# Layer 3 of a four-layer graph network: the product with W2 as seven products of halves, a mean by transposes, and adj's halves in three buffers

## The chip, the cores and the metric

The kernel runs on one core of a Trainium2 chip. The metric is the device time of one execution in microseconds, taken as the median of several runs. A core has a matrix engine (TensorE, PE in the profile; its weight loads are shown as PEld), VectorE (DVE), ScalarE (ACT), GpSimd (POOL) and SyncE (SP), which issues most transfers. All of them run at once, each through its own list of instructions in order, and wait for one another by semaphores. A matmul multiplies a stationary block of 128 x 128 (the weights) with a moving block of 128 rows and up to 512 columns, and its result goes to PSUM.

## The reference, cut to what matters

There are 16 graphs of 1024 nodes with 256 features each. Four layers follow one another, and each has the form x = x + layer(relu(layernorm(x)), adj). The change concerns the last one only:

```python
def _L3_gnn_ref(x, adjacency, epsilon, W1, b1, rms_weight, W2, b2):
    neighbor_sum = jnp.einsum('bnm,bmd->bnd', adjacency, x)
    agg = epsilon * x + neighbor_sum
    h = jnp.einsum('bnd,dh->bnh', agg, W1) + b1            # 256 -> 1024
    h = jax.nn.silu(_rmsnorm(h, rms_weight))               # over the 1024
    out = jnp.einsum('bnh,hd->bnd', h, W2) + b2            # 1024 -> 256
    return out
...
h = jnp.maximum(_layernorm(x, axis=-1), 0.0)
x = x + _L3_gnn_ref(h, adj, ...)
```

All data are fp32.

## The kernel before

Layers 0 and 1 work graph by graph and take the first 1443 us or so. Layer 2 is a recurrence over the nodes; it is written in an order fixed by hand, goes on until about 3392 us, and loads the first things for layer 3 on its way (`early_3`). Neither of them is touched. Layer 3 (`layer_3`) works through the 16 graphs ("batches") b = 0 to 15 from there to the end.

For one batch, layer 3 does this. `load(b)` fetches x, the result hn of layer 2 and the transposed adjacency matrix, the last in two halves of 512 columns (2 MB each, four transfers), all through SP's queue. `prepare(b)` adds hn to x, takes the layer norm's statistics on VectorE (lines 1150 to 1154), the power -1/2 on GpSimd (line 83, a helper), the Relu on ScalarE (line 1160), adds epsilon to the diagonal of adj (GpSimd, line 1141) and b2 to x (GpSimd, line 1164). `sums(b)` computes the neighbour sums, turned (features down, nodes across), in four parts of eight matmuls of 512 columns (line 1176). ScalarE copies each into `ag` (line 1178) and VectorE makes the differences `tt` (lines 1182 to 1186).

`inner` multiplies with W1. That product is already computed by the Strassen-Winograd scheme: both matrices are cut into 2 x 2 blocks, and seven products of blocks replace the eight. W1's sums of blocks are in `ws`; those of `ag` are in `tt`. For each of four k there are seven matmuls of 512 columns (line 1197). p1 goes from PSUM to SBUF on ScalarE (line 1212), VectorE adds it and the further products up in u2 and u3 (lines 1214 and 1216), and `result` adds the bias and writes a block of `hh` (line 1201). `result` also squares the block on ScalarE (line 1203, two `sq` buffers) and adds the square to `ss` on GpSimd (line 1205). The last product of a k is accumulated in PSUM on top of p5 and so has to wait until VectorE has read p5. `hh` is kept turned: the 1024 features are in 8 chunks of 128 partitions, nodes 0 to 511 in `hh[0]`, the others in `hh[1]`.

`norm` gives two steps. `mean` sums `ss` over the partitions by eight matmuls with one moving column of ones (line 1231, two records each) and gets the reciprocal root rms (lines 81 and 83). `spread` spreads rms over the partitions by eight transposes (line 1239), multiplies `hh` by it on VectorE (line 1242) and applies Silu on ScalarE (line 1243). `outer(b, hh, q)` multiplies one half of the nodes with W2: for each of four blocks of 128 nodes there are eight matmuls of 256 columns with the block of `hh` as weights (line 1251), and VectorE adds the result to x (line 1252). The store of x goes through GpSimd's queue (line 1282).

The loop at the end of `layer_3` sets the order: in iteration b come `load(b + 2)`, `inner` of b, the first part of `sums(b + 1)`, `mean`, the second part, `spread`, the third and fourth part, `outer` of the first half, `prepare(b + 2)`, `outer` of the second half, the store. Outside of layer 2 this is only the order in which the program is written. The framework's scheduler makes each engine's list from it and may move an instruction ahead of others that it doesn't depend on; `tc.issue_after(last)` keeps `prepare(b + 2)` from being put ahead of an add of `outer`.

Buffers: x has three, hn two, each half of adj has one of four (even batches use the two named `bxt`, odd ones the two named `at`), `hh[0]`, `hh[1]`, `ag` and `tt` have one each. PSUM has eight banks of 512 fp32 columns: five named `ph` (sums and `inner`), three named `po` (mean, spread, `outer`).

Of the kernel before, what the change touches and what calls it, by code (L numbers as in the profile page):

```python
# [9 lines left out]
F32 = mybir.dt.float32  # L10
# [6 lines left out]
P = 128  # L17
# [23 lines left out]
def gnn_stack(ctx: ExitStack, tc: tile.TileContext, a: dict, out: bass.AP):  # L41
# [1009 lines left out]


    def early_3(shared, pool, x, hn, at, h):

# [36 lines left out]
    def layer_3(shared, x, hn, at, h, eye):  # L1091
        with ExitStack() as st:
# [26 lines left out]
            nc.gpsimd.tensor_tensor(ws[:, 2], a12, ws[:, 1], ALU.subtract)  # L1119

            def load(b):
                if b:
# [6 lines left out]
                while len(at[b]) < N // NH:  # L1129
                    n0 = NH * len(at[b])  # L1130
                    half = shared.tile([P, NT, NH], F32, name="bxt") if b % 2 == 0 else big.tile([P, NT, NH], F32, name="at")
                    for t in range(0, NT, 2):
                        nc.sync.dma_start(half[:, t : t + 2], rows(a["adjT"][b])[:, t : t + 2, n0 : n0 + NH])
                    at[b].append(half)

            def prepare(b):
# [25 lines left out]
                to = x[b] if b else big.tile([P, NT, D], F32, name="x", bufs=3)  # L1162
                for t in range(NT):
                    nc.gpsimd.tensor_tensor(to[:, t], x[b][:, t], b2, ALU.add)  # L1164
                x[b] = to
# [23 lines left out]
            def inner(ag, tt):  # L1189
# [5 lines left out]
                def product(lhsT, rhs, onto=None):  # L1195
                    ph = onto if onto is not None else psum.tile([P, NH], F32, name="ph", bufs=5)
                    nc.tensor.matmul(ph, lhsT, rhs, start=onto is None, stop=True, skip_group_check=onto is not None)  # L1197
                    return ph

                def result(k, q, ph, u):  # L1200
# [5 lines left out]
                    begun[q] = True  # L1206

                for k in range(HH):
                    mine = slice(k * P, (k + 1) * P)
                    p1, u2, u3 = (small.tile([P, NH], F32, name=name) for name in ("p1", "u2", "u3"))  # L1210
                    ph = product(a11[:, mine], ag[:, 0, :NH])
                    nc.scalar.copy(p1, ph)  # L1212
                    ph = product(ws[:, 1, mine], tt[:, 1])
                    nc.vector.tensor_add(u2, ph, p1)  # L1214
# [5 lines left out]
                    result(k, 0, product(a12[:, mine], ag[:, 1, :NH]), p1)  # L1220
                    result(k, 1, product(ws[:, 2, mine], ag[:, 1, NH:], p5), u2)
                return hh, ss

            def norm(hh, ss):
# [3 lines left out]
                def mean():  # L1228
                    pq = psum.tile([P, N // P], F32, name="po", bufs=3)
                    for n in range(N // P):  # L1230
                        nc.tensor.matmul(pq[:, n : n + 1], ss[n // 4][:, n % 4 * P : (n % 4 + 1) * P], ones[:, 0:1],  # L1231
                                         start=True, stop=True)
                    got["rms"] = inv_sqrt(small, pq, RMS_EPS, [P, N // P], "rms", mul=1.0 / H)

# [10 lines left out]

            def outer(b, hh, q):
                for k in range(NH // P):
                    t = q * NH // P + k
                    po = psum.tile([P, D], F32, name="po", bufs=3)
                    for c in range(HC):  # L1250
                        nc.tensor.matmul(po, hh[q][:, c, k * P : (k + 1) * P], w2[:, c], start=c == 0, stop=c == HC - 1)  # L1251
                    last = nc.vector.tensor_add(x[b][:, t], x[b][:, t], po)
                return last.ins

# [7 lines left out]
            for b in range(B):  # L1262
# [12 lines left out]
                parts[3]()  # L1275
                last = outer(b, hh, 0)
                if b + 2 < B:

                    with tc.issue_after(last):
                        prepare(b + 2)  # L1280
                outer(b, hh, 1)
                nc.gpsimd.dma_start(rows(out[b]), x[b])
# [53 lines left out]
```

## Time and profile before

| | us |
|---|---|
| three runs | 4754.09, 4754.99, 4761.2 |
| median | 4754.99 |
| the profiled execution | 4754.82 |
| its span in the profile | 4753.1 |
| one batch of layer 3 in the middle | 83.07 |
| of it `inner`, sums with mean and spread, `outer` | 25.31, 30.13, 27.63 |
| mean granted TensorE clock over the span | 0.979 |

The profile describes one execution. Times in it are microseconds from the start of the span unless marked ns. A row of instructions gives line, engine, operation, what it writes and reads, the shape and the count. An fp32 matmul shows as two records of weight load and matmul (here called passes), a transpose as one. The end of a matmul is modelled, and neighbouring matmuls overlap in the records, so the distance from one start to the next says more than the duration. "Releaser" or "waited for" names the instruction that ended an engine's idle time.

### The profile page before, as it was taken

The numbers are of one execution on the slowest core, as the hardware profiler recorded it, in microseconds if no ns is written. First come the engines' busy times: TensorE is split into PE (matmuls) and PEld (weight loads), VectorE is DVE, ScalarE is ACT, GpSimd is POOL, SyncE is SP. The second block draws the span as 40 slices with busy tenths as digits, with TensorE's granted clock in tenths as the row PEclk, the third lists the DMA queues.
The fourth block names the chain that finished last, engine by engine and source line by source line (L and its number), as shares of the span: only waits on it lengthen the run. The fifth ranks groups of instructions, "written<-read, shape, count | busy, mean of one in ns | idle before, by whom it ended". The sixth has DMA issues, their size and how long they took to land. (4 is left out here: it accounts for less than half of the span.)

```text
span 4753.1 us, 52478 instructions
## 1 busy us (share of the span) xinstructions
PE 4421.1 (93%) x18071; PEld 2991.8 (63%) x18071; DVE 2344.1 (49%) x6436; ACT 1271.5 (27%) x2725; POOL 1554.1 (33%) x1926
## 2 busy tenths in 40 slices
PE   8998799999997989999999999998899999999998
PEld 4444455555554777777777777777556565565656
DVE  6667844446543444444444444445344444444443
ACT  1111112212211232222332323233233333333232
POOL 3213224334322323232223233324343424333331
PEclk9999899999998999999999999999899999999999
DMA  4333234654546443545344454431422232222200
GB/s 147 123 107 106 79 83 160 207 187 160 177 138 195 129 150 123 159 135 165 110 139 139 120 161 148 154 130 37 149 80 90 79 106 80 96 91 80 93 23 18
DMA packets 530981, 576.62 MB, mean 121 GB/s; under 512 B 42545, under 2 KB 439473, under 8 KB 528305
## 3 DMA queue, kind: packets, MB, share of 16 engines
q1 hardware_dynamic: 499536, 460.27, 31.3%
q0 software_dynamic: 31040, 111.44, 6.7%
q8 instruction: 196, 3.21, 0.3%
q14 instruction: 209, 1.70, 0.1%
HBM read 469.65 MB, written 116.65 MB: 123 GB/s over the span
## 5 line engine op out<-in xcount | busy, mean ns | idle before, releaser
L295 PE MATMUL pa<-at,h 128*128 128x512 f32 x1088 | 497.0, 610 | 32.9 <-DVE ag L300 32.9
L1251 PE MATMUL po<-w,hh 128*128 128x256 f32 x2048 | 447.6, 381 | 0.7 <-ACT hh L1243 0.7
L623 PE MATMUL pf<-hb,ab 128*128 128x256 f32 x1568 | 418.6, 385 | 28.1 <-DVE bxt L773 16.2
L1251 PEld LDWEIGHTS po<-w,hh 128*128 128x128 f32 x2048 | 391.0, 191 | 61.2 <-issue 7.2
L295 PE MATMUL pa<-at,q 128*128 128x512 f32 x960 | 424.4, 595 | 0.0
L295 PEld LDWEIGHTS pa<-at,h 128*128 128x128 f32 x1088 | 209.8, 196 | 278.8 <-issue 233.0
L735 PE MATMUL pf<-hs,wx 128*128 128x256 f32 x1536 | 350.2, 382 | 16.7 <-POOL hs L726 15.1
L1205 POOL TENSOR_TENSOR ss<-ss,sq 128x512 f32<-128x512 f32 x224 | 279.9, 1269 | 165.5 <-ACT sq L1203 161.7
L735 PEld LDWEIGHTS pf<-hs,wx 128*128 128x128 f32 x1536 | 291.3, 192 | 60.0 <-POOL hs L726 16.9
L623 PEld LDWEIGHTS pf<-hb,ab 128*128 128x128 f32 x1568 | 277.1, 192 | 67.8 <-DVE bxt L773 23.5
L295 PEld LDWEIGHTS pa<-at,q 128*128 128x128 f32 x960 | 178.3, 190 | 216.5 <-issue 212.6
L770 PE MATMUL pf<-bd,h 128*128 128x384 f32 (+5 forms) x768 | 213.9, 372 | 49.5 <-DVE bxt L773 26.5
L1022 POOL DMA_INDIRECT hs_d<-h,table x128 | 129.6, 1012 | 368.8 <-ACT gates L743 183.3
L1176 PE MATMUL ph<-bxt,hb 128*128 128x512 f32 x512 | 226.0, 597 | 4.0 <-ACT hb L1160 3.2
L1176 PE MATMUL ph<-at,hb 128*128 128x512 f32 x512 | 224.3, 593 | 0.0
L773 DVE TENSOR_TENSOR bxt<-bxt,pf 128x384 f32<-128x384 f32 (+5 forms) x384 | 141.3, 384 | 145.0 <-PE pf L770 124.8
L1242 DVE TENSOR_TENSOR hh<-hh,po 128x512 f32<-128x512 f32 x256 | 154.4, 679 | 111.6 <-PE po L1239 111.6
L83 POOL TENSOR_TENSOR rs<-rs_v,mhalf 128x8 f32<-128x8 f32 (+1 forms) x65 | 106.9, 1644 | 279.9 <-DVE rs_v L79 266.4
L740 DVE TENSOR_TENSOR gates<-pf,bias 128x512 f32<-128x512 f32 x128 | 88.3, 691 | 220.1 <-PE pf L735 205.4
L1203 ACT ACTIVATE sq<-hh 128x512 f32<-128x512 f32 x224 | 141.1, 630 | 194.8 <-DVE hh L1201 128.4
L770 PEld LDWEIGHTS pf<-bd,h 128*128 128x128 f32 x768 | 132.4, 192 | 94.4 <-DVE bxt L773 41.8
L829 ACT ACTIVATE r<-pr 128x256 f32<-128x256 f32 (+3 forms) x230 | 68.1, 348 | 405.8 <-PE pr L788 382.1
(274 smaller groups left out, 7917.4 us busy)
## 6 DMA issues: line engine op xcount, KB each, us to landing
at<-in_adjT SPq DMA_DIRECT2D x64, 1024.0 KB
ab<-in_adj SPq DMA_DIRECT2D x128, 512.0 KB
bxt<-in_adjT SPq DMA_DIRECT2D x64, 512.0 KB
at<-in_adjT SPq DMA_DIRECT2D x64, 512.0 KB
ad<-in_adj SPq DMA_DIRECT2D x128, 128.0 KB
x_d<-x POOLq DMA_DIRECT2D x16, 1024.0 KB, 4.8
he_d<-h POOLq DMA_DIRECT2D x16, 1024.0 KB, 9.2
heT_d<-hT POOLq DMA_DIRECT2D x16, 1024.0 KB
```

What stands on the lines that cost most here:

```text
L83: nc.gpsimd.tensor_tensor(r, t, mhalf.to_broadcast(shape), ALU.pow)
L295: nc.tensor.matmul(pa, h[:, mt, c * P : (c + 1) * P], at[n0 // 512][:, mt], start=mt == 0, stop=mt == NT - 1)
L623: nc.tensor.matmul(pb, ab[:, jts[k]], hb[:, jts[k]], start=k == 0, stop=k == len(jts) - 1)
L735: nc.tensor.matmul(pg[:, e], wx[:, c, q * D + e * P : q * D + (e + 1) * P], self.hs[:, c], start=c == 0, stop=c == DC - 1)
L770: nc.tensor.matmul(pf, h[:, g, c * P : (c + 1) * P], bd[:, g, b4 : b4 + 4, S : S + far], start=True, stop=True)
L773: return lambda: nc.vector.tensor_add(to, to, pf)
L1022: nc.gpsimd.indirect_dma_start(out=hs_d[t][g][:, :], out_offset=row(1, g, t, s), in_=h[:, g], in_offset=None)
L1176: nc.tensor.matmul(pa, h[b][:, mt, c * P : (c + 1) * P], at[b][n0 // NH][:, mt], start=mt == 0, stop=mt == NT - 1)
L1203: nc.scalar.activation(sq, hh[q][:, k], AF.Square)
L1205: nc.gpsimd.tensor_tensor(ss[q], ss[q], sq, ALU.add)
L1242: nc.vector.tensor_mul(hh[q][:, k], hh[q][:, k], pr)
L1251: nc.tensor.matmul(po, hh[q][:, c, k * P : (k + 1) * P], w2[:, c], start=c == 0, stop=c == HC - 1)
```

## The change

The change has five parts.

1. `outer` handles both halves of the nodes together, as a 2 x 2 block product with seven products of blocks. A block of `hh` is 512 features by 512 nodes, a block of W2 is 512 features by 128 columns. W2's sums of blocks (`wt`, and v12 in place) are made once by four GpSimd instructions. The sums of `hh`'s blocks are made per batch on VectorE (`combine`, eight instructions of 1024 columns), three of them in place and one in a new buffer `s1`. A product is 16 matmuls of 128 columns. Results go to x from PSUM on VectorE (four adds of 512 columns) or by way of `p1`, `u2` and `u3` (one copy on ScalarE, two adds on VectorE, three on GpSimd).
2. `mean` turns `ss` by eight transposes into PSUM and sums with two VectorE reductions.
3. In `inner` the last product of a k, with its `result`, is written after the first product and the copy of p1 of the next k (`left`).
4. The 32 halves of adj go round three buffers (two `bxt`, one `at`) instead of four.
5. `prepare(b + 2)` is issued after the add of the third product in `outer`, and its b2 add takes two blocks at a time.

The diff, without a blank line that it adds near the top:

```diff
--- before.py
+++ after.py
@@ -1118,6 +1119,13 @@
             nc.gpsimd.tensor_tensor(a21, a11, a21, ALU.subtract)
             nc.gpsimd.tensor_tensor(ws[:, 2], a12, ws[:, 1], ALU.subtract)
 
+            wt = wp.tile([P, 3, HH, P], F32, name="wt")
+            v11, v12, v21, v22 = (w2[:, m * HH : (m + 1) * HH, e * P : (e + 1) * P] for m in range(2) for e in range(2))
+            nc.gpsimd.tensor_tensor(wt[:, 0], v12, v11, ALU.subtract)
+            nc.gpsimd.tensor_tensor(wt[:, 1], v22, wt[:, 0], ALU.subtract)
+            nc.gpsimd.tensor_tensor(v12, v22, v12, ALU.subtract)
+            nc.gpsimd.tensor_tensor(wt[:, 2], v21, wt[:, 1], ALU.subtract)
+
             def load(b):
                 if b:
                     x[b] = big.tile([P, NT, D], F32, name="x", bufs=3)
@@ -1128,7 +1136,11 @@
                     at[b] = []
                 while len(at[b]) < N // NH:
                     n0 = NH * len(at[b])
-                    half = shared.tile([P, NT, NH], F32, name="bxt") if b % 2 == 0 else big.tile([P, NT, NH], F32, name="at")
+
+                    if (2 * b + len(at[b])) % 3 < 2:
+                        half = shared.tile([P, NT, NH], F32, name="bxt")
+                    else:
+                        half = big.tile([P, NT, NH], F32, name="at", bufs=1)
                     for t in range(0, NT, 2):
                         nc.sync.dma_start(half[:, t : t + 2], rows(a["adjT"][b])[:, t : t + 2, n0 : n0 + NH])
                     at[b].append(half)
@@ -1160,8 +1172,8 @@
                     nc.scalar.activation(h[b][:, t], x[b][:, t], AF.Relu, bias=shift[:, k : k + 1], scale=rs[:, k : k + 1])
                 diagonal(1)
                 to = x[b] if b else big.tile([P, NT, D], F32, name="x", bufs=3)
-                for t in range(NT):
-                    nc.gpsimd.tensor_tensor(to[:, t], x[b][:, t], b2, ALU.add)
+                for t in range(0, NT, 2):
+                    nc.gpsimd.tensor_tensor(to[:, t : t + 2], x[b][:, t : t + 2], b2[:, None].to_broadcast([P, 2, D]), ALU.add)
                 x[b] = to
 
             def sums(b):
@@ -1205,11 +1217,13 @@
                         nc.gpsimd.tensor_tensor(ss[q], ss[q], sq, ALU.add)
                     begun[q] = True
 
+                left = lambda: None
                 for k in range(HH):
                     mine = slice(k * P, (k + 1) * P)
                     p1, u2, u3 = (small.tile([P, NH], F32, name=name) for name in ("p1", "u2", "u3"))
                     ph = product(a11[:, mine], ag[:, 0, :NH])
                     nc.scalar.copy(p1, ph)
+                    left()
                     ph = product(ws[:, 1, mine], tt[:, 1])
                     nc.vector.tensor_add(u2, ph, p1)
                     ph = product(a21[:, mine], tt[:, 2])
@@ -1218,7 +1232,9 @@
                     result(HH + k, 1, p5, u3)
                     result(HH + k, 0, product(a22[:, mine], tt[:, 3]), u3)
                     result(k, 0, product(a12[:, mine], ag[:, 1, :NH]), p1)
-                    result(k, 1, product(ws[:, 2, mine], ag[:, 1, NH:], p5), u2)
+                    left = lambda k=k, mine=mine, p5=p5, u2=u2: result(
+                        k, 1, product(ws[:, 2, mine], ag[:, 1, NH:], p5), u2)
+                left()
                 return hh, ss
 
             def norm(hh, ss):
@@ -1226,11 +1242,13 @@
                 got = {}
 
                 def mean():
-                    pq = psum.tile([P, N // P], F32, name="po", bufs=3)
-                    for n in range(N // P):
-                        nc.tensor.matmul(pq[:, n : n + 1], ss[n // 4][:, n % 4 * P : (n % 4 + 1) * P], ones[:, 0:1],
-                                         start=True, stop=True)
-                    got["rms"] = inv_sqrt(small, pq, RMS_EPS, [P, N // P], "rms", mul=1.0 / H)
+                    all_ = small.tile([P, N // P], F32, name="all")
+                    for q in range(2):
+                        pq = psum.tile([P, NH // P, P], F32, name="po", bufs=3)
+                        for n in range(NH // P):
+                            nc.tensor.transpose(pq[:, n], ss[q][:, n * P : (n + 1) * P], ident)
+                        nc.vector.tensor_reduce(all_[:, q * NH // P : (q + 1) * NH // P], pq, AX.X, ALU.add)
+                    got["rms"] = inv_sqrt(small, all_, RMS_EPS, [P, N // P], "rms", mul=1.0 / H)
 
                 def spread():
                     for q in range(2):
@@ -1243,14 +1261,54 @@
                             nc.scalar.activation(hh[q][:, k], hh[q][:, k], AF.Silu, scale=rw[:, k : k + 1])
                 return mean, spread
 
-            def outer(b, hh, q):
-                for k in range(NH // P):
-                    t = q * NH // P + k
-                    po = psum.tile([P, D], F32, name="po", bufs=3)
-                    for c in range(HC):
-                        nc.tensor.matmul(po, hh[q][:, c, k * P : (k + 1) * P], w2[:, c], start=c == 0, stop=c == HC - 1)
-                    last = nc.vector.tensor_add(x[b][:, t], x[b][:, t], po)
-                return last.ins
+            def outer(b, hh, then):
+
+
+                a11, a12, a21, a22 = (hh[q][:, m * HH : (m + 1) * HH] for q in range(2) for m in range(2))
+                x11, x12, x21, x22 = (x[b][:, q * 4 : (q + 1) * 4, e * P : (e + 1) * P] for q in range(2) for e in range(2))
+
+                def combine(to, left, right, op):
+                    for c in range(0, HH, 2):
+                        nc.vector.tensor_tensor(to[:, c : c + 2], left[:, c : c + 2], right[:, c : c + 2], op)
+
+                def product(left, right, onto=None):
+                    po = onto if onto is not None else psum.tile([P, NH // P, P], F32, name="po", bufs=3)
+                    for n in range(NH // P):
+                        for c in range(HH):
+                            nc.tensor.matmul(po[:, n], left[:, c, n * P : (n + 1) * P], right[:, c],
+                                             start=onto is None and n == 0 and c == 0, stop=c == HH - 1, skip_group_check=True)
+                    return po
+
+                def partial(name, *sources):
+                    t = small.tile([P, NH // P, P], F32, name=name)
+                    if len(sources) == 1:
+                        nc.scalar.copy(t, sources[0])
+                    else:
+                        nc.vector.tensor_add(t, *sources)
+                    return t
+
+                s1 = big.tile([P, HH, NH], F32, name="s1", bufs=1)
+                po = product(a11, v11)
+                p1 = partial("p1", po)
+                combine(s1, a21, a22, ALU.add)
+                combine(a21, a11, a21, ALU.subtract)
+                product(a12, v21, po)
+                nc.vector.tensor_add(x11, x11, po)
+                combine(a11, s1, a11, ALU.subtract)
+                combine(a12, a12, a11, ALU.subtract)
+                po = product(a22, wt[:, 2])
+                last = nc.vector.tensor_add(x21, x21, po)
+                with tc.issue_after(last.ins):
+                    then()
+                p5 = product(s1, wt[:, 0])
+                nc.vector.tensor_add(x22, x22, p5)
+                u2 = partial("u2", product(a11, wt[:, 1]), p1)
+                nc.gpsimd.tensor_tensor(x12, x12, u2, ALU.add)
+                u3 = partial("u3", product(a21, v12), u2)
+                nc.gpsimd.tensor_tensor(x21, x21, u3, ALU.add)
+                nc.gpsimd.tensor_tensor(x22, x22, u3, ALU.add)
+                product(a12, v22, p5)
+                nc.vector.tensor_add(x12, x12, p5)
 
             load(0)
             prepare(0)
@@ -1273,12 +1331,8 @@
                 spread()
                 parts[2]()
                 parts[3]()
-                last = outer(b, hh, 0)
-                if b + 2 < B:
-
-                    with tc.issue_after(last):
-                        prepare(b + 2)
-                outer(b, hh, 1)
+
+                outer(b, hh, (lambda: prepare(b + 2)) if b + 2 < B else (lambda: None))
                 nc.gpsimd.dma_start(rows(out[b]), x[b])
 
     layers_0_1()

```

## The prediction

> **What bounds the kernel now.** I read the page's busy shares first, then the timeline of TensorE in one late batch of layer 3, then a table of three stages of one batch, and last the waits between 3572 and 4652 us, where thirteen batches run alike. TensorE is busy for 93% of the span:
>
> ```profile
> PE 4421.1 (93%) x18071; PEld 2991.8 (63%) x18071; DVE 2344.1 (49%) x6436; ACT 1271.5 (27%) x2725; POOL 1554.1 (33%) x1926
> ```
>
> The timeline (start, duration, engine, line, count) shows a batch as one unbroken string: sums, the 16 passes of the mean, sums, 8 transposes, sums, and then the 128 passes of `outer` with W2:
>
> ```profile
> 4626.89 1.84 PE L1231 MATMUL po<-ones,ss 128*128 128x1 f32 x16
> 4628.59 7.11 PE L1176 MATMUL ph<-at,hb 128*128 128x512 f32 x16
> 4635.54 1.04 PE L1239 MATMUL po<-ident,rms 128*128 128x128 f32 x8
> 4636.42 13.90 PE L1176 MATMUL ph<-at,hb 128*128 128x512 f32 x32
> 4650.15 27.79 PE L1251 MATMUL po<-w,hh 128*128 128x256 f32 x128
> 4677.78 1.02 PE L1197 MATMUL ph<-ag,w 128*128 128x512 f32 x2
> ```
>
> Every matmul is two records ("passes"), every transpose one. The stage table (stretch, its length, busy time of the engines, TensorE clock, DMA) of another batch has `inner`, the sums with mean and spread, and `outer`:
>
> ```profile
> 4096.29:4121.60 25.31, 24.56 (x57) 10.47 (x56) 16.42 (x24) 10.46 (x18) 14.59 (x14) 1.00 0.25 83
> 4121.60:4151.73 30.13, 30.13 (x89) 14.77 (x88) 11.38 (x20) 13.19 (x22) 8.23 (x9) 1.00 0.19 70
> 4151.73:4179.36 27.63, 27.63 (x129) 24.32 (x128) 10.56 (x32) 4.63 (x9) 7.83 (x12) 1.00 0.33 115
> ```
>
> A batch takes 83.07 us at full clock, and TensorE fills all of it but about 1.3 us in `inner`. In `outer` VectorE is busy for only 10.6 of 27.6 us: room for work. The waits (who, for whom, total, times, longest) name the hole in `inner`:
>
> ```profile
> DVE u L1214 <- ACT p L1212: 76.9, 39, 2.6
> ACT sq L1203 <- POOL ss L1205: 52.3, 77, 0.8
> PE ph L1197 <- DVE hh L1201: 8.3, 14, 0.6
> ```
>
> GpSimd's adds hold back a square on ScalarE (two sq buffers), the p1 copy is queued behind it, VectorE waits for p1, and TensorE's last product, which goes onto p5, waits until VectorE has read p5.
>
> **What the Trainium skill says.** TensorE: Matmul & The Clock Gate, section LDWEIGHTS: a load takes its columns / 1.2 ns, 107 ns for 128 (an estimate from that page); section Back-to-back issue gap: the spacing is set by load and matmul together. Here 16 passes of one column last 1.84 us, (1.84 - 0.167) / 15 = 0.111 us apart (0.167 us is the shortest record of that group): the trace agrees, although the load's own row says 190 ns. VectorE: DVE Perf Modes, section on the errata: an fp32 tensor_tensor takes (N + 151) / 0.96 ns: 691 at 512, where this trace has 692 (L1214), and 1224 at 1024, which the trace shows only with broadcast operands (L418, 1368). The same page's table of perf modes has no faster mode for tensor_reduce; the trace's row of 512 elements from PSUM (L209) took 674 ns.
>
> **The W2 product.** Removed: 64 matmuls of 256 columns, 128 passes in 27.63 us, 0.216 each. Added: seven products of 16 matmuls of 128 columns, 224 passes, each with its own weights. Regular fp32 matmuls of this shape stand in layer 2:
>
> ```profile
> 2419.48 1.05 PE L788 MATMUL pr<-dx,wh 128*128 128x128 f32 x8
> 2420.37 1.06 PE L788 MATMUL pz<-dx,wh 128*128 128x128 f32 x8
> ```
>
> 0.89 us for eight, 0.111 us a pass, the same as with one column. 224 x 0.111 = 24.9 us: 2.7 us less a batch. Seven eighths would be 24.2 us; the rest goes to the load's pace.
>
> Whether TensorE is fed: let T be the start of the last two sums, 13.7 us before `outer`. VectorE multiplies hh until T+9.3, and the Silus end at T+10.7 (4148.9 in the batch above, T = 4138.16). Then come, in the compiled order, a tt subtraction, s1 (two of 1024 elements; 1.14 us each if they overlap as the 512s do, 0.60 apart; 1.22 by the page; 1.37 at worst), two for a21, three tt, two for a11, two for a12. s1 is done at T+12 to 13; TensorE needs it after three products, 3 x 3.55 = 10.7 us into `outer`, T+24.4. The a11 combination waits for the first product to be read (T+17.4), ends by T+20 and is due at T+28; a12 waits for the second (T+21.9), ends by T+25 and is due at T+35. PSUM's three po buffers come free at T+24 (x11 add) and T+25.5 (x21 add), wanted at T+28 and T+31.5. So about 9.5 us of combinations, the four adds and two partials of 0.69 (before: eight adds of 0.42) fall in VectorE's idle time. Were that cover gone, each microsecond too late would cost one a batch, 16 in all.
>
> One tight place: the second product goes onto the PSUM that ScalarE copies to p1 (0.59 us; I take L1178's row). The compiled order puts four of a22's matmuls between, 8 x 0.111 = 0.89 us, against about 0.16 of drain, 0.59 of copy and 0.1 of signals. Bounds 0 (hidden) and 0.85 (all exposed); I take 0.1 a batch.
>
> **prepare(b+2)** starts after the third product, not between the halves. It issues no DMA. Its VectorE work, 6.1 us before, runs T+25.5 to T+32; queued behind it are the x22 add (due for the seventh product, T+35) and u2. The power on GpSimd ends at T+34.3, eight Relus at T+38.4, and ScalarE's next duty is the p1 copy at T+39.7. GpSimd then has three new adds (3 x 1.27 us), the four double-width b2 adds (1.27 to 1.46 us for what were 2 x 0.73) and the store, until about T+44.5; the next ss add is due at T+45.5. Cost taken: 0, bounds 0 and 1 us a batch; the store moves by some 4 us, and x, which SP loads behind it, is wanted a batch later.
>
> **Mean.** 16 passes (1.71 us from start to start) become 8 transposes, which at line 1239 take 0.88: 0.83 us less. Two reductions (0.69 each) are added between them and the power, while TensorE runs 6.9 us of sums; rms was ready about 4 us before its use, so they are hidden, in all batches but the last.
>
> **Order in inner.** The last product of a k moves behind the next first one, and p1's copy ahead of the fourth square. By the 0.859 us of a product, VectorE has read p5 at 5.3 us after that k's first product begins, and TensorE writes it at 6.9; p1 done 1.5 us late would still do. 25.31 becomes 28 x 0.859 = 24.05 and I leave 0.1: 1.15 us less. Bounds: 0 and 1.26.
>
> **adj in three buffers.** In the compiled order of SP, batch b+2's second half goes out once the first two sums of iteration b have read the old one, and batch b+3's first half after the last two: 2 MB each, where before each group came with that timing too, a half ahead. The landing is due at TensorE a batch later; on GpSimd the diagonal adds stand ahead of the power. They ended at T+25 (4163.2 + 0.9) before and the power is due at T+32.6. Cost 0, bounds 0 and 1 us.
>
> **W2's differences** (four GpSimd adds, 1.27 us each, once) lie in a stretch where GpSimd idles 10.6 us before a power: 0. wt and s1 take the room of one buffer.
>
> **Sum.** 2.7 - 0.1 + 0.83 + 1.15 = 4.6 us a batch, 83.07 to 78.5. Fifteen batches: 69. In the last nothing covers the spread: there I walked the same chain from 4713.4 us (start of the multiplications): the last add ends near 4743 instead of 4746.2, and inner, mean and a shorter ss chain give some 2 more: 5. Together 74, against the profiled execution's 4754.82 us (span 4753.1 and 1.7 around it; the median of the runs is 4754.99): 4681.
>
> **Rivals.** *A wait stays or comes* in each batch: p5's wait in `inner` not removed (1.15), or the p1 copy, a combination or GpSimd late by about as much. For it: four engines are now booked tightly in `outer`. Against: the margins above. 16 x 1.2 = 19: 4700. *Slower*: passes with their own weights at the 190 ns of the load's row. 224 x 0.190 = 42.6 us, 17.7 more a batch: 4681 + 283 = 4964. It decides from (24.9 + 4.6) / 224 = 0.132 us a pass. Against it: 0.111 in two places. *adj late*: a half that lands over 8 us later than before holds the power, and over some 10 the sums; 16 x 2 = 32: 4713. *Better than forecast*: TensorE without any wait and a shorter tail: 4672.
>
> **Numbers.** Forecast 0.70 (own range 4675 to 4688), a wait 0.16, slower 0.04, adj late 0.03, better 0.07. The range of 4671 to 4710 takes in the wait and half of the better case and leaves out about 0.1. Faster by over 0.2% (9.5 us, about what a measurement of this kernel can tell from no change) 0.95, within it 0.01, slower 0.04.
>
> **What would show it.** Right: 224 passes of 128 columns in about 25 us from first to last; transposes of ss in 0.9 us; no wait of line 1209 for VectorE; a batch of 78.5 us. Wrong: passes over 0.12 us apart, line 1278 waiting for ScalarE or VectorE, or sums waiting for GpSimd or DMA.

## The result, and the profile after

| | before | after |
|---|---|---|
| median of four runs, us | 4756.94 | 4685.06 |
| the profiled execution | 4754.82 | 4692.98 |
| one batch of layer 3 in the middle | 83.07 | 78.32 |
| of it `inner`, sums with mean and spread, `outer` | 25.31, 30.13, 27.63 | 24.04, 29.22, 25.06 |
| layer 3, from its first sums to its last add | 1354.1 | 1281.2 |

The ratio is 0.985, with a 95% interval of 0.9832 to 0.9867: faster, by about 72 us. The forecast was 4681. The two profiled executions are only 62 us apart, because in that of after layer 3's first sums start at 3402.66 us, in that of before at 3392.10, though layers 0 to 2 are the same code. In the thirteen traces of this document this start lies anywhere between 3385 and 3405 us, so below I compare layer 3 with layer 3, and one batch with one batch.

The busy shares of the page of after: TensorE is still the full engine, with more instructions in less time, and VectorE has taken on 208 us.

```profile
PE 4365.5 (93%) x19479; PEld 2999.7 (64%) x19479; DVE 2551.8 (54%) x6564; ACT 1280.5 (27%) x2741; POOL 1622.2 (35%) x1914
```

The timeline of TensorE over one batch of after (start, duration, line, count):

```profile
4101.73 1.04 PE L1249 MATMUL po<-ident,ss 128*128 128x128 f32 x8
...
4110.35 13.90 PE L1188 MATMUL ph<-bxt,hb 128*128 128x512 f32 x32
4124.09 3.73 PE L1278 MATMUL po<-w,hh 128*128 128x128 f32 x32
4127.66 1.06 PE L1278 MATMUL po<-wt,hh 128*128 128x128 f32 x8
4128.55 3.79 PE L1278 MATMUL po<-w,hh 128*128 128x128 f32 x32
4132.17 2.84 PE L1278 MATMUL po<-wt,hh 128*128 128x128 f32 x24
4134.85 3.74 PE L1278 MATMUL po<-wt,s 128*128 128x128 f32 x32
4138.43 3.74 PE L1278 MATMUL po<-wt,hh 128*128 128x128 f32 x32
4142.00 7.31 PE L1278 MATMUL po<-w,hh 128*128 128x128 f32 x64
4149.15 1.02 PE L1209 MATMUL ph<-ag,w 128*128 128x512 f32 x2
```

From 4124.09 to 4149.15 stand 224 passes, 25.06 / 224 = 0.112 us each, where 128 wider ones stood before. No row names a releaser: TensorE waits for nobody. The stage table of this batch (stretch, its length, busy time of PE, PEld, DVE, ACT and POOL, TensorE clock, DMA) says the same, since PE is busy for the whole length of each stage:

```profile
4070.83:4094.87 24.04, 24.04 (x59) 10.65 (x58) 17.40 (x24) 10.87 (x19) 18.74 (x16) 1.00 0.26 88
4094.87:4124.09 29.22, 29.22 (x82) 13.81 (x81) 16.28 (x26) 12.82 (x21) 7.62 (x9) 1.00 0.21 72
4124.09:4149.15 25.06, 25.06 (x226) 25.06 (x225) 17.90 (x35) 5.12 (x10) 7.94 (x9) 1.00 0.36 126
```

In `outer` VectorE went from 10.6 to 17.9 us busy and the records of the weight loads (PEld) now cover all of the stage. Such a record is 190 ns long and the next load starts 112 ns later, so the cover by itself doesn't say that the loads set the pace; the run with half of the columns (below) is about that. The waits from 3650 to 4600 us no longer have a row in which line 1209 or 1278 of TensorE waits for another engine. What is left in `outer` is ScalarE and VectorE waiting for TensorE, the harmless direction, as here (who, for whom, total, times, longest):

```profile
DVE hh L1272 <- PE po L1278: 33.9, 25, 2.2
```

### The profile page after: what moved, and what is told of

The parts are those of the page before. It is cut to its first block, busy times and chain, and to the rows that moved or that the text cites. A ratio compares the mean times of both kernels' runs of the same rounds, so it can differ in the third digit from the quotient of the medians.

```text
span 4691.1 us, 55474 instructions
## 1 busy us (share of the span) xinstructions
PE 4365.5 (93%) x19479; PEld 2999.7 (64%) x19479; DVE 2551.8 (54%) x6564; ACT 1280.5 (27%) x2741; POOL 1622.2 (35%) x1914
## 5 line engine op out<-in xcount | busy, mean ns | idle before, releaser
L735 PEld LDWEIGHTS pf<-hs,wx 128*128 128x128 f32 x1536 | 290.4, 191 | 62.8 <-POOL hs L726 19.9
L1188 PE MATMUL ph<-bxt,hb 128*128 128x512 f32 x704 | 309.3, 595 | 3.9 <-ACT hb L1172 3.1
L1278 PEld LDWEIGHTS po<-w,hh 128*128 128x128 f32 x2048 | 236.2, 193 | 9.5 <-issue 7.2
L1278 PE MATMUL po<-w,hh 128*128 128x128 f32 x2048 | 240.3, 277 | 1.4 <-ACT hh L1261 0.7
L1188 PEld LDWEIGHTS ph<-bxt,hb 128*128 128x128 f32 x704 | 132.6, 191 | 163.9 <-issue 159.0
```

The lines of the kernel that those rows point to most:

```text
L735: nc.tensor.matmul(pg[:, e], wx[:, c, q * D + e * P : q * D + (e + 1) * P], self.hs[:, c], start=c == 0, stop=c == DC - 1)
L1188: nc.tensor.matmul(pa, h[b][:, mt, c * P : (c + 1) * P], at[b][n0 // NH][:, mt], start=mt == 0, stop=mt == NT - 1)
L1278: nc.tensor.matmul(po[:, n], left[:, c, n * P : (n + 1) * P], right[:, c], start=onto is None and n == 0 and c == 0, stop=c == HH - 1, ski ...
```

## The experiments: one part undone at a time

My theory was that each of three parts (products, order, mean) pays for itself, by itself, and that the buffers pay nothing.

**Old `outer`.** The whole of `outer` and its call are those of before, `wt` is gone:

```diff
-                outer(b, hh, (lambda: prepare(b + 2)) if b + 2 < B else (lambda: None))
+                last = outer(b, hh, 0)
+                if b + 2 < B:
+                    with tc.issue_after(last):
+                        prepare(b + 2)
+                outer(b, hh, 1)
```

> The changed kernel with its new mean, order and adj buffers, but W2's product as 64 matmuls of 256 columns again (128 passes), the eight wide adds on VectorE, no differences of W2, and the next-but-one batch's LayerNorm between the halves. My theory, that the gain of outer is the number and pace of passes and nothing else of the batch depends on it: outer 27.6 us instead of 25.06, a batch 78.32 + 2.57 = 80.9 us, about 41 us more in all than the changed kernel, near 4726. Rival, that part of the gain comes from the work moved off the wide adds or from the later LayerNorm: inner or the sums change too and the total differs from +41 by 10 us or more.

Measured: 4723.59 us median; a batch 80.88 us, layer 3 1319.4. The timeline has the old string of wide passes back:

```profile
4137.77 27.79 PE L1262 MATMUL po<-w,hh 128*128 128x256 f32 x128
4165.39 1.02 PE L1202 MATMUL ph<-ag,w 128*128 128x512 f32 x2
```

27.62 instead of 25.06: +2.56 a batch, and no other stage moved. Over 16 batches that would be 41; layer 3 shows 38.2, because the part after the last `inner` gives 0.5 us and not 2.56, and the head of layer 3 (up to the end of its first `inner`) got 0.8 us shorter without `wt`; both come back below. The theory stands, with the place of `prepare` undone along with the products; the rival wanted a change elsewhere in the batch and there is none.

**Old order in `inner`.**

```diff
...
-                    left()
...
-                    left = lambda k=k, mine=mine, p5=p5, u2=u2: result(
-                        k, 1, product(ws[:, 2, mine], ag[:, 1, NH:], p5), u2)
-                left()
+                    result(k, 1, product(ws[:, 2, mine], ag[:, 1, NH:], p5), u2)
```

> The changed kernel with each k's seventh product of inner directly after the sixth again, so that p5 is written again at once. My theory: TensorE's wait for VectorE's read of p5 comes back, inner goes from 24.04 to about 25.3 us, a batch to 79.6, about 20 us more in all, near 4705; the waits name line 1209 of TensorE behind the u add or its PSUM. Rival: the wait went because GpSimd and ScalarE have other loads now (the squares' queue), so the order is worth nothing: within 3 us of the changed kernel.

Measured: 4706.05 us; a batch 79.61, +1.29; layer 3 1302.5, +21.3. The wait is back; two rows of TensorE's timeline at the end of an `inner`, and the row of the waits from 3650 to 4600 us:

```profile
4103.81 1.02 PE L1209 MATMUL ph<-ag,w 128*128 128x512 f32 x2
4105.43 1.12 PE L1209 MATMUL ph<-ag,ws 128*128 128x512 f32 x2 [0.60 <-DVE hh L1213]
```

```profile
PE ph L1209 <- DVE hh L1213: 9.2, 24, 0.6
```

From start to start 1.62 us where a product takes 0.86. The bracket says 0.60, since the modelled end of the matmul before reaches into the gap: the distance of the starts says what was lost, 0.76 here, some 0.3 at the third k, and 0.1 behind each (0.96 to the next start instead of 0.86). All else of the change is in place in this run, so it is the order that removes the wait, and not the changed work of the other queues.

**Old mean.**

```diff
...
-                        for n in range(NH // P):
-                            nc.tensor.transpose(pq[:, n], ss[q][:, n * P : (n + 1) * P], ident)
-                        nc.vector.tensor_reduce(all_[:, q * NH // P : (q + 1) * NH // P], pq, AX.X, ALU.add)
+                    for n in range(N // P):
+                        nc.tensor.matmul(pq[:, n : n + 1], ss[n // 4][:, n % 4 * P : (n % 4 + 1) * P], ones[:, 0:1],
+                                         start=True, stop=True)
...
```

> The changed kernel with the mean of squares as 16 passes with a column of ones again. My theory: 1.71 us of TensorE instead of 0.88 in each batch and two reductions less on VectorE; a batch 78.32 + 0.83 = 79.2 us, about 13 us more in all, near 4698. Rival: the sums around it were also shortened by the transposes (29.22 against 30.13 us measured, 0.91), or the reductions delay the multiplications: then the difference is not 0.8 a batch but nearer 0.3 or 1.2 (5 or 19 us in all).

Measured: 4698.27 us; a batch 79.22, +0.90; layer 3 1294.9, +13.7. The 16 passes stand in the timeline again, 1.70 us from their start to the next start:

```profile
4178.03 1.84 PE L1247 MATMUL po<-ones,ss 128*128 128x1 f32 x16
4179.73 7.11 PE L1188 MATMUL ph<-at,hb 128*128 128x512 f32 x16
```

0.82 of the 0.90 is that; the sums behind it end some 0.08 us later too (7.11 against 7.03 in the row). The three parts add up: 2.56 + 1.29 + 0.90 = 4.75, and 83.07 - 78.32 is 4.75. Within these readings nothing is lost or won between them.

**Two buffers for adj.**

```diff
-                    if (2 * b + len(at[b])) % 3 < 2:
-                        half = shared.tile([P, NT, NH], F32, name="bxt")
-                    else:
-                        half = big.tile([P, NT, NH], F32, name="at", bufs=1)
+                    half = shared.tile([P, NT, NH], F32, name="bxt")
```

> The changed kernel with adj's halves in two buffers instead of three, so that a half can be loaded only after the sums of the one before it in its buffer. My theory: the half lands about 8 us before it is needed on GpSimd and more before TensorE's use, so no change: 78.3 us a batch, total within 3 us of the changed kernel, 4685. Rival, that the third buffer hides a late landing: the diagonal adds and the power behind them on GpSimd are late, 1 to 2 us a batch, 16 to 32 in all, near 4701 to 4717, with sums of TensorE that wait for GpSimd or a DMA.

Measured: 4690.07 us (ratio to before 0.9855, interval 0.9836 to 0.9875, the same as after's); a batch 78.31; layer 3 1280.6. The second half now lands a little later, and nobody is hurt. GpSimd in one batch, T (the start of the last two sums) being 4105.71:

```profile
4127.14 3.66 POOL L1150 TENSOR_TENSOR bxt<-bxt,eye 128x128 f32<-128x128 f32 x4 [15.77 <-DMA bxt<-in_adjT]
4137.55 1.65 POOL L83 TENSOR_TENSOR rs<-rs_v,mhalf 128x8 f32<-128x8 f32 x1 [6.76 <-DVE rs_v L79]
```

The diagonal adds end at T+25.1 (in after at T+23.8) and the power still waits 6.76 us for VectorE. Three buffers and two are worth the same; the cost of 0 in the prediction holds for even less room than the change has.

## The experiments: what paces a pass, and how full VectorE is

**Half of the columns** in each of W2's products; the other half of the result is left out.

```diff
-                    po = onto if onto is not None else psum.tile([P, NH // P, P], F32, name="po", bufs=3)
+                    po = onto if onto is not None else psum.tile([P, NH // P, P // 2], F32, name="po", bufs=3)
...
-                            nc.tensor.matmul(po[:, n], left[:, c, n * P : (n + 1) * P], right[:, c],
+                            nc.tensor.matmul(po[:, n], left[:, c, n * P : (n + 1) * P], right[:, c, : P // 2],
```

> The changed kernel with 64 of the 128 columns in each of W2's seven products, and the partial sums and adds to x half as wide: half of the columns of W2's product are left out. Theory, that a pass waits for its own weights: passes stay 0.111 us apart and outer lasts 24.9 us. Rival, that a pass is paced by the columns that it moves: 0.055 to 0.06 us apart, 224 of them in 12.5 to 14 us, where VectorE's combinations would then be late.

Measured: a batch of 78.27 us. Two products of 32 passes each in the timeline:

```profile
4125.65 3.74 PE L1278 MATMUL po<-wt,s 128*128 128x64 f32 x32
4129.22 3.74 PE L1278 MATMUL po<-wt,hh 128*128 128x64 f32 x32
```

3.57 us for 32 passes, 0.112 each, as with 128 columns. Half of the work saved 0.05 us a batch. With the one column of the old mean a pass took 0.111 us too. So up to 128 columns the pace doesn't depend on the columns; what these passes share is that each loads its own 128 columns of weights. The Trainium skill's section LDWEIGHTS (page TensorE: Matmul & The Clock Gate) gives the time of a load as its columns / 1.2 ns, which makes 107 ns here, an estimate from that page; the measured pace is within 5 ns of it. That the load is what sets the pace is an inference from this agreement. It also says why seven products of eight gave 2.57 of 27.63 us (9%) and not an eighth: at 256 columns a pass took 0.216, at 128 it took 0.112 and not 0.108. The one run took 4703.05 us for another reason, told in the last section.

**More work on VectorE**: the combination s1 computed three times instead of once, and in another run, which came first, five times.

```diff
                 combine(s1, a21, a22, ALU.add)
+                combine(s1, a21, a22, ALU.add)
+                combine(s1, a21, a22, ALU.add)
```

> The changed kernel with the combination s1 computed three times over: four more additions of 1024 elements on VectorE, 4.7 us a batch, nothing left out. With 9.4 us more a batch took 80.44 us instead of 78.32. My theory: VectorE's stalls absorb some 3 us and the rest moves the LayerNorm by under 2 us, inside the margin of ScalarE and GpSimd ahead of the next inner's squares: 78.3 to 78.5 us a batch. Rival, that the cost is in proportion: 79.4 us a batch, 17 in all.

Measured: a batch of 78.31 us: 4.7 us more on VectorE cost nothing in it. The run took 4697.21 us, and layer 3 is 4.3 longer than in after, 3.5 of it after the last `inner`. In the last `outer` no LayerNorm is left that could be put off, and TensorE waits for s1 and what follows:

```profile
4670.46 0.68 PE L1278 MATMUL po<-wt,s 128*128 128x128 f32 x4 [1.59 <-DVE s L1272]
4671.50 3.39 PE L1278 MATMUL po<-wt,s 128*128 128x128 f32 x28 [0.36 <-DVE s L1272]
4675.60 0.68 PE L1278 MATMUL po<-wt,hh 128*128 128x128 f32 x4 [0.70 <-DVE hh L1272]
```

> The changed kernel with the combination s1 computed five times over instead of once: eight more additions of 1024 elements on VectorE, 9.4 us a batch, nothing left out. My theory, that VectorE has some 3 us of waiting and the rest of its room in outer: two of its stalls, 2.8 us, take part of it, the LayerNorm of the next-but-one batch moves by 6.3 us, the fourth and fifth products wait for x22's turn and the next inner for its p1 copy behind late Relus: about 4 us a batch, 55 in all, near 4740. Rival, that VectorE's booking in outer is tight: all of the 9.4 us show, 140 in all, near 4825. Another, that the work is hidden: 4685.

Measured: 4721.95 us; a batch of 80.44 us, +2.12, half of what I expected; layer 3 1320.3. The fourth and fifth products of `outer` didn't wait, against what I had thought (line 1278 of TensorE waits for 0.4 us in all from 3500 to 4600): in the compiled order, products of the next `inner` stand ahead of a part of the fifth and of the seventh. The time went where the LayerNorm's lateness arrives, in `inner` by way of ScalarE and GpSimd. TensorE, then ScalarE:

```profile
4174.94 1.12 PE L1209 MATMUL ph<-tt,w 128*128 128x512 f32 x2 [1.38 <-ACT p L1225]
```

```profile
4160.94 4.05 ACT L1172 ACTIVATE hb<-x,shift,rs 128x256 f32<-128x256 f32 x8 [11.62 <-DVE shift L1170]
...
4171.23 0.63 ACT L1215 ACTIVATE sq<-hh 128x512 f32<-128x512 f32 x1 [3.67 <-POOL ss L1217]
```

The Relus end at T+46 instead of T+38.9 (T is 4118.97 here), GpSimd's b2 and ss adds follow them late, a square waits 3.67 us for GpSimd, the p1 copy stands behind the squares, and TensorE loses 1.5 us at once. The chain of the old `inner` comes back through another door. The margin of a batch in after is thus between 4.7 and 9.4 us of VectorE's time, and by these rows it ends in GpSimd's queue, not at VectorE's busy share.

## The experiments: the head of layer 3

The forecast was 4 us off, less than the runs differ among themselves, but two terms of the sum were visibly wrong, and one could be mended. In the first `inner` TensorE waits for `tt`; first the row of before, then three of after:

```profile
3430.47 2.05 PE L1197 MATMUL ph<-tt,ws 128*128 128x512 f32 x2 [4.63 <-DVE tt L1184]
```

```profile
3435.26 1.02 PE L1209 MATMUL ph<-ag,w 128*128 128x512 f32 x2
3442.61 2.04 PE L1209 MATMUL ph<-tt,ws 128*128 128x512 f32 x2 [6.33 <-DVE tt L1196]
3444.45 1.91 PE L1209 MATMUL ph<-tt,w 128*128 128x512 f32 x2
```

The chain, from the timelines of GpSimd, SP (after, then before) and ScalarE:

```profile
3418.99 1.27 POOL L1127 TENSOR_TENSOR wt<-w,wt 128x512 f32<-128x512 f32 x1
3420.21 4.94 POOL L1176 TENSOR_TENSOR x<-hb,b 128x512 f32<-128x512 f32 x4
```

```profile
3425.18 0.37 SPq L1134 DMA_DIRECT2D hb<-hn_d  x1
```

```profile
3412.93 0.37 SPq L1126 DMA_DIRECT2D hb<-hn_d  x1
```

```profile
3439.20 2.07 ACT L1172 ACTIVATE hb<-x,shift,rs 128x256 f32<-128x256 f32 x4 [10.02 <-DVE shift L1170]
3441.18 0.56 ACT L1190 COPY ag<-ph 128x512 f32<-128x512 f32 x1
```

W2's four differences stand ahead of batch 0's b2 adds. These read the buffer into which SP is to load hn of batch 1; the load goes out 22.5 us after layer 3's first sums, 20.8 before. Batch 1's statistics follow, and four of its Relus stand ahead of the ag copy that `tt` needs. I tried two edits, together and alone:

```diff
-            nc.gpsimd.tensor_tensor(wt[:, 0], v12, v11, ALU.subtract)
+            nc.vector.tensor_tensor(wt[:, 0], v12, v11, ALU.subtract)
...
-                nc.vector.scalar_tensor_tensor(shift, mv[:, part, 0], -1.0, rs, op0=ALU.mult, op1=ALU.mult)
+                with tc.issue_after(hold) if hold is not None else ExitStack():
+                    nc.vector.scalar_tensor_tensor(shift, mv[:, part, 0], -1.0, rs, op0=ALU.mult, op1=ALU.mult)
...
-                part()
-            prepare(1)
+                last = part()
+            prepare(1, last.ins)
```

Both edits, with the changed kernel once more beside them:

> The changed kernel once more, for a time on the same chip as the three below. Expected: 4685 us, within 6 of it; a batch of layer 3 of 78.3 us.

> The changed kernel with W2's four differences on VectorE instead of GpSimd, and the LayerNorm shift of batch 1 held back until the last combination of tt, so that ScalarE copies ag before that batch's Relus. My theory, that the first inner waits for tt because the differences on GpSimd delay the bias add, with it a load, and so those Relus on ScalarE: TensorE's 6.3 us wait at the head falls to 0 to 2 us, 4 to 6 us less in all, near 4680; the batches after it unchanged. Rival: the Relus that now come later delay the squares of the first inner on ScalarE or the diagonal adds, and the time comes back there: within 2 us of the changed kernel.

> One half of the earlier head experiment: W2's four differences on VectorE instead of GpSimd, the LayerNorm of batch 1 not held. From the start of layer 3's first sums to the second inner product it took 38.4 us in the kernel before, 39.95 in the changed kernel, 35.7 with both edits. Theory, that the differences on GpSimd cost this head 1.6 us and the rest of the wait is the Relus' own place ahead of the ag copy: 38.4 us here, TensorE's wait 4.6 to 5 us. Rival, that the differences are the whole cause of the wait: below 36.5.

> The other half: the shift of batch 1 held until the last tt, the differences left on GpSimd. Theory: the ag copy no longer stands behind four Relus, whose delay then doesn't matter to TensorE: 35.7 to 36 us from the first sums to the second inner product, nearly no wait of TensorE, as with both edits; layer 3 some 7 us shorter than in the changed kernel (1281.2 us). Rival: VectorE's statistics of batch 1, late through the load, still stand ahead of tt: 37 to 38 us.

| us | before | after | again | both | differences on VectorE | held only |
|---|---|---|---|---|---|---|
| TensorE's wait in the first `inner` | 4.63 | 6.33 | 6.33 | 0.63 | 2.26 | 0.64 |
| first sums to first product of `inner` | 32.7 | 32.6 | 32.6 | 34.0 | 34.1 | 36.0 |
| first sums to second product of `inner` | 38.4 | 39.95 | 39.99 | 35.7 | 37.4 | 37.6 |
| first sums to end of the first `inner` | 64.7 | 65.7 | 65.9 | 58.9 | 62.3 | 60.9 |
| layer 3 | 1354.1 | 1281.2 | 1281.4 | 1273.7 | 1277.2 | 1275.4 |

A batch in the middle is 78.3 us in all four of the kernels after. Both edits: 4680.31 us (ratio to before 0.9831, interval 0.9816 to 0.9845), the changed kernel beside it 4690.36 (0.9851, 0.9837 to 0.9864). The intervals overlap, so the medians alone don't prove it; in the traces layer 3 is 7.5 and 7.7 us shorter than in the two of the changed kernel, 6.8 and 7.0 of it up to the end of the first `inner`, and that part is the one that was edited. It is the best version I have.

The single runs took 4671.57 and 4684.4 us, mostly by how early layer 3 began, and are read by the table. With the differences on VectorE the load goes out at 19.9 us, 2.6 earlier than in after, and the second product comes 2.6 earlier too: it follows the load by 17.4 to 17.5 us in before, after and this run, so it is the load that the head hangs on. It even goes out 0.9 earlier than in before: the bias that the b2 adds wait for landed 0.6 earlier, and the adds, two blocks at a time, are 0.3 shorter. The other 1.5 of the 4.1 us by which the wait shrank is no gain: TensorE itself came later, since its first sums took longer in this run (the row above the second product, and below). 37.4 lies between my two expectations, so neither "1.6 us" nor "the whole cause" is right. Held alone, the wait for `tt` is gone as expected, but 37.6 is not the 35.7 to 36 that I wrote: the first sums waited 5.00 us for ScalarE's first Relu in that run (2.93 with both edits). The load ahead of this Relu went out 7.9 us after the first sums (5.8 with both edits), ahead of anything that the edit moves, so that run's transfers are the likelier cause; one run can't settle it.

What I had not written down is the second line of the price: the wait cools TensorE. The table of stretches of after, and of the version with both edits (the eighth number is the clock):

```profile
3435.20:3442.60 7.40, 1.08 (x3) 0.21 (x2) 2.94 (x13) 3.40 (x7) 3.89 (x5) 0.88 1.07 364
3442.60:3448.60 6.00, 5.99 (x8) 2.54 (x9) 3.06 (x5) 1.59 (x4) 4.36 (x5) 0.58 1.07 376
```

```profile
3435.90:3439.40 3.50, 3.47 (x8) 1.62 (x9) 3.16 (x6) 2.28 (x6) 1.10 (x2) 1.00 1.03 335
```

The same eight passes take 6.0 us at a clock of 0.58 and 3.5 at 1.00. The wait of 6.33 us cost 2.5 us more after it was over; a wait of 0.63 costs nothing more. The Trainium skill's page TensorE: Matmul & The Clock Gate (What's actually happening) has this as a halved clock after an idle window of about 3.4 us. The wait of 6.33 agrees; but with the differences on VectorE a wait of 2.26 us was followed by two slow products as well (1.84 and 1.63 us from start to start instead of 0.86), so 3.4 is no safe bound here.

How near this is to chance is seen in the first sums, which contain one wait for ScalarE in every kernel. In twelve of the thirteen traces it is 2.76 to 3.18 us long (5.00 in the one with the hold alone). Behind it the next 46 passes take 20.01 us in six of the twelve and 21.70 in the other six (with both edits the clock stands at 0.50 from 3415 to 3417 us, in after at 1.00 from 3415.4 on). The same wait of 2.87 us was followed by either, in the run with the old `outer` and in that with half of the columns:

```profile
3409.14 21.70 PE L1181 MATMUL ph<-bxt,hb 128*128 128x512 f32 x46 [2.87 <-ACT hb L1165]
```

```profile
3405.01 20.01 PE L1188 MATMUL ph<-bxt,hb 128*128 128x512 f32 x46 [2.87 <-ACT hb L1172]
```

In the table, before, after and its repetition had the fast sums and the three edited kernels slow ones (21.45 us with the hold alone). With both edits the second product follows the first by 1.65 us, so with fast sums this head would be up to 1.7 us shorter still, an estimate from these rows.

## Why the prediction was right, step by step

- **W2 product, 2.7 less 0.1 a batch.** Measured 2.57 (2.56 by the run with the old `outer`). 224 passes at 0.111 to 0.112 us. The 0.1 for the p1 copy wasn't needed in a batch in the middle: the copy (0.59 us) ends at 4128.45 and the product onto that PSUM starts at 4128.55, where the eight passes of a22 put it anyway.
- **Whether TensorE is fed.** The walk held to within 1 us, most of it to a few tenths. T is 4110.35; Silus end at T+10.9 (forecast 10.7), s1 at T+12.3 (12 to 13), a11 at T+19.4 (20), a12 at T+24.9 (25), x11's add at T+23.7 (24), the power at T+33.6 (34.3), the Relus at T+38.9 (38.4), GpSimd's store is issued by T+44.3 (44.5). The two places where VectorE waits for a block to be read, and GpSimd's first ss add, which still waits for ScalarE and not the other way round:

```profile
4127.41 2.36 DVE L1272 TENSOR_TENSOR hh<-s,hh 128x1024 f32<-128x1024 f32 x2 [0.62 <-PE po L1278]
4131.93 1.47 DVE L1272 TENSOR_TENSOR hh<-hh 128x1024 f32<-128x1024 f32 x1 [2.15 <-PE po L1278]
```

```profile
4153.73 0.94 POOL L1336 DMA_DIRECT2D out<-x  x1
4156.06 1.26 POOL L1217 TENSOR_TENSOR ss<-ss,sq 128x512 f32<-128x512 f32 x1 [1.40 <-ACT sq L1215]
```

- **Readings of before.** Some readings in the walk were off without harm. T of the batch in the prediction is 4138.00 and not 4138.16, so the Silus ended at T+10.9 there already. The diagonal adds of before ended at T+26, not T+25. rms was ready 4.9 us before its use, not 4. And 1368 ns for line 418 is a mean that a few long ones pull up: its median is 1223 ns, the figure of the formula.
- **Mean 0.83, order 1.15.** Measured 0.90 and 1.27 to 1.29: the 0.1 left in `inner` wasn't needed, and `inner` is 28 products of 0.859 us without a gap.
- **adj's buffers, 0.** Confirmed, even with two. **The move of `prepare`, 0**: it was not run alone, but it lies inside the margin that 4.7 us of extra VectorE work didn't use up.
- **Sum of a batch, 4.6.** Measured 4.75: the order gave 0.12 more than forecast, the mean 0.07. 15 batches from the end of the first `inner` to the end of the last gave 71.6 us, not 69.
- **Last batch, 5, and the head, not in the sum.** Here the sum was mis-sized: both together measured 1.2. After the last `inner` layer 3 got 2.25 us shorter, of which 1.0 in the chain of squares and mean (with one more `inner` it was to be some 2); the last `outer` with its spread gave only 1.3 instead of about 3. Its first product runs cold, and the p1 copy, which no pass of a22 covers there, is waited for:

```profile
4653.90 6.74 PE L1278 MATMUL po<-w,hh 128*128 128x128 f32 x32 [0.68 <-ACT hh L1261]
4661.32 3.84 PE L1278 MATMUL po<-w,hh 128*128 128x128 f32 x32 [0.68 <-ACT p L1285]
```

  The cold start was there before too (its 128 passes took 30.71 us, 2.9 more than in the middle, against 3.0 here), so it cancels; the 0.68 us for the copy and an add twice as wide at the very end (0.69 for 0.42 us) don't. That one more `inner`, 1.15, is the first one when batches are counted from its end; and the head with it became 1.0 us longer.
- **W2's differences, 0.** This step failed. The idle of 10.6 us that was to cover them is there, but it comes after the b2 adds; the differences were queued ahead of those, and behind the b2 adds stands a load. They cost 1.7 us of waiting, and the passes behind the longer wait lost 2.6 us at the lower clock where those behind the wait of before lost 1.7. 71.6 + 1.2 = 72.85 (rounded) against the forecast of 74: that the total fits so well is in part luck, since the batches gave 2.6 us more than forecast and the two ends 3.8 less.
- **The rivals.** Passes at the 190 ns of the load's row: refuted, that row is a duration and loads overlap. A wait that stays, adj late: none in the trace. *Better than forecast* came true by half: TensorE has no wait in a batch, but the tail is not shorter than forecast.

## What to carry to other kernels

A scheme that trades multiplications for additions and narrows the passes pays only by what a pass then takes: here 0.11 us at full clock for every fp32 pass of up to 128 columns with weights of its own. Count with that, and get the additions into the idle time of another engine by walking due times (in `outer` all came out within 1 us here). One-time set-up work needs the same walk: look at what stands behind it in its own queue, loads that wait for a buffer included, not at the idle time of the engine's row. And a wait of TensorE of 6 us costs more than it lasts, since the passes behind it run cold.

## What the runs showed of the hardware that I had not expected

The run with half of the columns ended its last batch at half clock. TensorE was busy but for one gap of 0.46 us and never came back to full clock; its table of stretches, and for comparison that of after, whose passes have 128 columns:

```profile
4644.60:4659.00 14.40, 13.94 (x63) 13.51 (x63) 10.18 (x16) 8.92 (x15) 0.00 (x0) 0.50 0.00 0
4659.00:4672.00 13.00, 13.00 (x62) 13.00 (x63) 7.40 (x8) 0.00 (x0) 0.00 (x0) 0.50 0.00 1
```

```profile
4653.90:4657.50 3.60, 3.60 (x14) 3.26 (x15) 3.60 (x7) 3.60 (x7) 0.00 (x0) 0.50 0.00 0
4657.50:4661.00 3.50, 3.14 (x20) 2.95 (x19) 3.50 (x7) 1.57 (x4) 0.00 (x0) 0.73 0.00 0
4661.30:4665.00 3.70, 3.68 (x33) 3.69 (x34) 1.39 (x3) 3.70 (x7) 0.00 (x0) 1.00 0.00 0
```

With 128 columns the clock is back some 5 us after the product's start; with 64 it stayed at 0.50 for 49 us, to the end of the kernel, though in the batches in the middle, which come to it warm, the same passes kept a clock of 1.00. In this state a pass takes 0.213 us, twice 0.107. Over the 224 passes that makes some 20 us, as much as this run's layer 3 (1301.4 us) is longer than after's. The two runs differ here in the columns that a pass moves, not in how busy TensorE is; but one run shows it, I did not test it, and what the clock goes by stays open. Back to back, VectorE's additions of 1024 elements came every 1.13 to 1.18 us, though each lasts 1.22 by its record, which is also what the formula of the Trainium skill's page VectorE: DVE Perf Modes (the section on the errata) gives for one: a gain too small to decide anything here.
